# Graph layers on one Trainium2 core: each chunk's products right behind its copied sums, its bias added beside the square, and new limits for where conversions are placed

## The chip, the cores and the metric

The kernel runs on one core of a Trainium2 chip. A core has five engines with queues of their own, each worked off in order: TensorE (PE, matrix products into PSUM), VectorE (DVE), ScalarE (ACT), GpSimd (POOL), and SyncE (SP), which here only issues DMA transfers. Engines wait for each other by semaphores. The metric is the device time of one execution in microseconds (us), the median of several runs.

## The reference, cut to what matters

```python
# x: 4096 x 64; adj: 4096 x 4096, mostly zero, with the diagonal set
h = relu(layernorm(x))
for k in range(2):                       # first layer, two hops
    agg = adj @ h
    h = tanh(concat([agg, h], 1) @ W[k])
x = x + h

h = relu(layernorm(x))                   # second layer
support = h @ weight
mask = adj != 0
rank = cumsum(mask, axis=1); deg = rank[:, -1:]
k = minimum(deg, 100); pos = rank - (deg - k)
w = mask * where(pos > 0, 0.5 ** (k - pos), 0)
out = x + w @ support + bias
```

The adjacency is needed as numbers three times: in the first hop, in the second hop, and as the weights w of the second layer, which depend only on where its nonzeros stand.

## The kernel before, in words

The 4096 nodes are 32 blocks of 128, and the blocks make four chunks (numbered 0 to 3) of eight. A 512 KB block of the adjacency is 128 source nodes by the 1024 target nodes of a chunk, in fp32.

**First sweep** (`sweep1`, until about 202 us). All blocks are loaded; PE sums the first hop, and VectorE and ScalarE turn each block into one byte per entry ("codes"), from which the weight of the second layer can be computed later. A code becomes final when the counts of its row are known; `settle` (L392, L396) subtracts them for four blocks at once.

**Second sweep** (`sweep2`, L756). The second hop needs 72 of the blocks again. They go through a ring of six slots of one block, from the 21st block on through four (L803 to L806). SyncE issues the transfer of a block (L814) when PE has given up its slot, and PE adds it with two products (`agg_pair`, L256). The 36 steps of the loop take two blocks each: four of chunk 2, eight of chunk 3 (blocks 5 to 12), twelve of chunk 2 (13 to 24), 24 of chunk 1 (25 to 48), 24 of chunk 0 (49 to 72). `lasts` names the last block of each chunk. Then `finish_x2` (L536) makes the input of the second layer from a chunk's sums, in stages that are separated by `yield`:

1. ScalarE copies the sums from PSUM (S, L540), and SyncE loads the residual (xres, L542);
2. PE multiplies S by the hop's weights (py, L548), VectorE adds the other half (y, L554), ScalarE takes tanh (L558);
3. VectorE adds the residual (L561) and forms mean and difference (L189, L190), ScalarE squares (L191);
4. VectorE sums the squares (L193, L194), and GpSimd takes the power of -0.5 (L195);
5. VectorE scales (L198) and splits the result in a high and a low half (L582, L583), which are the features; GpSimd adds the bias for the output to `pre1` (L587).

Beside this runs **the second layer** in 128 units. A unit is a conversion of one block of codes into fp32r weights and two products with the features (`layer1`, L695). ScalarE converts with one instruction (Exp, L656) and VectorE with two (L648, L651). A conversion needs a free buffer for its weights, and takes one that an earlier unit has given up; at first there are only a few. The units of chunk 3 come first, then those of chunks 2, 1 and 0. Full sums are moved out of PSUM into `parts` (L724, L727, L730), and at the end multiplied by the layer's weight and added to `pre1` (`finish_out`, L746, L751), and stored (L753).

**What sets the order.** The order on each engine is written out when the program is built. A planner keeps a clock for each engine, in us, with a fixed cost for each operation (`use`). `chain` holds the chunk that is being finished and the time of its next stage; `run_chain` issues a stage once PE's clock has reached that time. `decode` (L660) places conversions on ScalarE as long as its clock is less than `lead` (5.0) ahead of PE's, on VectorE up to `dlead`, and settles in between. Where a chunk is being finished and more than three converted blocks are in stock, a conversion has to end within 0.4 of the chunk's next stage. `fill` and the loop's end place units where their features and weights are ready by the clocks. The last 56 units stand behind the last block (`n_late`), with the finishing of chunk 0 among them.

Of the kernel before, what the change touches and what calls it, by code (L numbers as in the profile page):

```python
# [16 lines left out]
ALU = mybir.AluOpType  # L17
AX = mybir.AxisListType

P = 128  # L20
# [23 lines left out]
def gnn_kernel(  # L44
# [20 lines left out]
    nc = tc.nc  # L65

    D = x.shape[-1]
# [3 lines left out]
    CB = 8  # L71
# [26 lines left out]
    pre1 = cpool.tile([P, NB, D], F32, name="pre1")  # L98
# [44 lines left out]
    bias_b = wb[:, HOPS * 2 + 1, :]  # L143
# [240 lines left out]
    settled = []  # L384
# [112 lines left out]
    clock = {"PE": 0.0, "DVE": 0.0, "ACT": 0.0, "POOL": 0.0, "DMA": 0.0}  # L497

    def use(engine, us, after=0.0):
        clock[engine] = max(clock[engine], after) + us  # L500
        return clock[engine]
# [33 lines left out]

    def finish_x2(I, acc):  # L536

        h = chunk(I)
        S = tmp(name="S")
        nc.scalar.copy(S, acc)  # L540
        xres = tmp([P, CB, D], name="xres")
        nc.sync.dma_start(xres, x[I])  # L542
        yield use("ACT", 0.6, clock["PE"] + 0.2) + 0.1

        pt = one(name="py")
        v = by_t(S)
        for t in range(TC):
            nc.tensor.matmul(  # L548
                pt[:, t * P : (t + 1) * P].rearrange("p (c e) -> p c e", c=NC),
                v[:, t // 2, t % 2, :], wz[:, :, 1, 0, :],  # L550
                start=True, stop=True, skip_group_check=True,
            )
        y = tmp([P, CB, D], name="y")
        nc.vector.tensor_tensor(  # L554
            as_nodes(y), pt.rearrange("p (t c e) -> p t c e", t=TC, c=NC), as_nodes(pre1[:, h, :]),
            op=ALU.add,
        )
        nc.scalar.activation(y, y, AF.Tanh)  # L558
        t = use("DVE", 0.7, use("PE", 1.15) + 0.2)
        yield use("ACT", 0.65, t + 0.1) - 0.5  # L560
        nc.vector.tensor_add(pre1[:, h, :], xres, y)  # L561
        t = use("DVE", 0.7, clock["ACT"] + 0.1)
        ln = ln_relu(None, pre1[:, h, :])
        next(ln)
        t = use("DVE", 1.4, t)
        yield use("ACT", 0.65, t + 0.1)
        next(ln)
        t = use("DVE", 0.9, clock["ACT"])
        yield use("POOL", 1.8, t + 0.1)
        try:  # L570
            next(ln)
        except StopIteration as stop:
            h2 = stop.value
        t = use("DVE", 0.9, clock["POOL"])
        if I == NCH - 1:
            feats[I] = feats[1] = place([P, CB, 2 * D], F32R, "mbuf", "feat")
        elif I == 0:
            feats[I] = feats[2]
        assert I > 1 or state["done"] >= CB * NCH * (2 - I)
        assert I != 2 or not any(w is lent[2] for w, _ in made[state["done"] :])  # L580
        hi, lo = feats[I][:, :, :D], feats[I][:, :, D:]
        nc.vector.tensor_scalar(hi, h2, SCALE, None, op0=ALU.mult)  # L582
        nc.vector.scalar_tensor_tensor(  # L583
            lo, h2, SCALE, hi.bitcast(F32), op0=ALU.mult, op1=ALU.subtract
        )
        ready[I] = use("DVE", 1.2, t + 0.1) + 0.2
        nc.gpsimd.tensor_tensor(  # L587
            pre1[:, h, :], pre1[:, h, :],
            bias_b[:, None, :].to_broadcast([P, CB, D]), op=ALU.add,
        )  # L590

# [29 lines left out]
    units = [(J, g, n) for J in range(NCH - 1, -1, -1) for g in order[J] for n in range(CB)]  # L623
    sums = {}
    parted = set()
    ready = {}
    made = []
    done = {}
    chain = []
    state = {"done": 0, "lead": 5.0, "dve": False, "dlead": 1.0, "free": 0.0}  # L630

    def convert(engine=None):
        i = len(made)
# [26 lines left out]
    def decode():  # L660
        while True:
            ahead = len(made) - state["done"]
            now = clock["PE"] + state["lead"]

            end = max(chain[0][0], clock["PE"]) + 0.4 if chain and ahead > 3 else 1e9
            t = min((v[1] for v in spaces), default=1e9)
            act, dve = (max(clock[e], t) for e in ("ACT", "DVE"))
            if len(made) == len(units):
                act = dve = 1e9
            if state["dve"] and dve + 1.4 < act + 1.05 and dve <= min(max(clock["PE"] + state["dlead"], state["free"]), end - 1.4):  # L670
                convert("DVE")
            elif act <= min(now, end - 1.05):
                convert("ACT")
            elif settled and clock["DVE"] <= clock["PE"] + 1.5 and (
                not chain or max(clock["DVE"], clock["PE"]) <= max(chain[0][0], clock["PE"]) + 0.3
            ):
                J, g, s = settled[0]
                settle()
                done[J, g] = use("DVE", 1.25)
            else:  # L680
                return

    def layer1(n):

        for i in range(state["done"], min(state["done"] + n, len(units))):
            state["done"] += 1
            while len(made) <= i:
                convert()
            J, g, k = units[i]
            if k == 0 and g not in sums:  # L690
                sums[g] = pacc.tile([P, NC, C], F32, tag="acc", name="accl")
            first, last = k == 0 and (J + 1, g) not in kept, k == CB - 1 and (J, g) not in kept
            w = made[i][0]
            for c in range(NC):
                nc.tensor.matmul(  # L695
                    sums[g][:, c, :], feats[J][:, k, :], w[:, c * C : (c + 1) * C],
                    start=first, stop=last,
                )
            space(w, use("PE", 0.45, max(made[i][1], ready[J])) + 0.2)
            if k < CB - 1:  # L700
                continue
            t = clock["PE"] + 0.2

            if (J, g) == (NCH - 1, 1):

                give_back("bits")
                state["dve"] = True
            if 0 < J < NCH - 1 or J and g % 2:
                pair_space(f"code{g}{J}", t)
            elif J:  # L710
                parts[g // 2] = place([P, 2, NC, C], F32, f"code{g}{J}", "parts")
            if (J, g) in kept:
                continue
            t = evict(J, g, sums.pop(g))
            if J == 0:
                outs.append((t + 0.1, partial(finish_out, g, part(g))))
# [39 lines left out]
    def sweep2(acc):  # L756
# [8 lines left out]
        free = {s: 3.5 * (n // 2 - 2) for n, s in enumerate(ring_all)}  # L765
# [7 lines left out]
        def run_chain(now):  # L773
            if chain and chain[0][0] <= now:
                t, gen = chain.pop(0)
                t = next(gen, None)
                if t is not None:
                    chain.insert(0, (t, gen))
                return True
            return False  # L780
# [20 lines left out]
        for n in range(0, total, 2):  # L801
            I, b = blocks[n]
            if n == 20:  # L803
                slots = ring_all[2:4] + ring_all[:2]
                seq = 0
                pair_space(f"ring{rings[2]}", *(free[s] for s in ring_all[4:]))  # L806
            if I not in accs:
                accs[I] = two(name="acc1") if I == 1 else plow.tile([P, C], F32, tag="low", name="acc1")
            fill(slots[seq % len(slots)])
            for r in range(2):  # L810
                s = slots[seq % len(slots)]
                seq += 1
                a = ring[s[0]][:, s[1], :]
                nc.sync.dma_start(a, adjA[I, NB - 1 - b - r])  # L814
                landed = use("DMA", 1.33, free[s]) + 2.2
                agg_pair(accs[I], at(b + r)[:, D:], a, (I, b + r) == firsts[I], (I, b + r) == lasts[I])
                free[s] = use("PE", 0.9, landed)
            next(last, None)
            if (I, b) == (2, NB - 2):
                give_back(I)  # L820
            if (I, b + 1) == lasts[I]:
                gen = finish_x2(I, accs[I])
                chain.append((next(gen), gen))
            run_chain(clock["PE"])
            if I == 0:

                state["lead"] = min(10.0, 1.1 * (total - 3 - n))
            decode()
            while state["done"] < min(due(n + 2) + 6, len(units) - n_late):
                i = state["done"]  # L830
                J = units[i][0]
                if J not in ready or max(ready[J], made[i][1] if len(made) > i else 1e9) > clock["PE"] + 0.3:
                    break
                layer1(1)
                run_chain(clock["PE"])
                decode()
# [64 lines left out]
```

## Time and profile before

| | |
|---|---|
| median of three runs | 372.81 us (371.53 to 374.83) |
| profiled execution, its own time | 370.68 us |
| span of its instructions | 368.8 us |
| PE busy | 338.8 us (92%) |
| VectorE busy | 293.0 us (79%) |
| ScalarE busy | 200.9 us (54%) |
| GpSimd busy | 24.6 us (7%) |
| DMA | 108.45 MB, mean 294 GB/s |
| granted TensorE clock | 1.0 |

The profile is of one execution. A row of the timeline gives start and length in us, engine, source line, operation, what it writes and reads with shape and type, how many instructions were merged, and in brackets how long the engine was idle before and what ended that. PE's fp32 products are recorded twice each: x4 of L256 is one block. Ends of PE's rows are modelled and overlap the next start a little, so the time of work in a run is taken from start to start. A row of the waits gives the engine and line that waited, what released it, and the sum, number and longest of these waits.

### The profile page before, as it was taken

The numbers are of one execution on the slowest core, as the hardware profiler recorded it, in microseconds if no ns is written. First come the engines' busy times: TensorE is split into PE (matmuls) and PEld (weight loads), VectorE is DVE, ScalarE is ACT, GpSimd is POOL, SyncE is SP. The second block draws the span as 40 slices with busy tenths as digits, with TensorE's granted clock in tenths as the row PEclk, the third lists the DMA queues.
The fourth block names the chain that finished last, engine by engine and source line by source line (L and its number), as shares of the span: only waits on it lengthen the run. The fifth ranks groups of instructions, "written<-read, shape, count | busy, mean of one in ns | idle before, by whom it ended". The sixth has DMA issues, their size and how long they took to land. (4 is left out here: it accounts for less than half of the span.)

```text
span 368.8 us, 3974 instructions
## 1 busy us (share of the span) xinstructions
PE 338.8 (92%) x1356; PEld 151.4 (41%) x1356; DVE 293.0 (79%) x522; ACT 200.9 (54%) x227; POOL 24.6 (7%) x21
## 2 busy tenths in 40 slices
PE   3787789999999999999999989799999999989996
PEld 0142224333343444534444422143355534447585
DVE  4998999399989999979989866688458629948993
ACT  2277981675167350650002424158969499939991
POOL 2221100000000000000000000312000030003000
PEclk9999999999999999999999999999999999999999
DMA  8999999999995978739999889978985698820002
GB/s 300 411 410 406 407 410 406 411 410 407 409 400 150 378 297 334 287 121 367 294 306 350 314 299 412 336 283 305 311 303 184 226 335 283 289 96 0 2 29 85
DMA packets 29827, 108.45 MB, mean 294 GB/s; under 512 B 2416, under 2 KB 2800, under 8 KB 29808
## 3 DMA queue, kind: packets, MB, share of 16 engines
q1 hardware_dynamic: 29808, 108.21, 79.3%
q8 instruction: 10, 0.16, 0.2%
q14 instruction: 9, 0.07, 0.0%
HBM read 107.15 MB, written 1.05 MB: 293 GB/s over the span
## 5 line engine op out<-in xcount | busy, mean ns | idle before, releaser
L656 ACT ACTIVATE weights<-codes,zero 128x1024 fp32r<-128x1024 uint8 x93 | 98.5, 1138 | 5.7 <-PE accl L695 5.2
L256 PE MATMUL acc<-ring,hx 128*64 128x512 f32 x288 | 71.6, 608 | 8.8 <-DMA ring<-in_adjA_dram 8.6
L695 PE MATMUL accl<-weights,feat 128*128 128x512 f32 x254 | 67.6, 407 | 1.4 <-DVE weights L651 1.0
L468 PE MATMUL acc<-ring,hx 128*128 128x512 f32 x152 | 66.1, 593 | 0.0
L256 PE MATMUL acc_low<-codes,hx 128*64 128x512 f32 x224 | 53.4, 598 | 7.9 <-DMA codes<-in_adjA_dram 7.9
L695 PEld LDWEIGHTS accl<-weights,feat 128*128 128x128 f32 x254 | 44.9, 188 | 29.2 <-ACT weights L656 13.4
L468 PEld LDWEIGHTS acc<-ring,hx 128*128 128x128 f32 x152 | 28.7, 190 | 37.1 <-issue 36.5
L250 DVE TENSOR_SCALAR cnt<-codes 128x512 uint16<-128x512 uint16 x128 | 37.7, 294 | 4.4
L249 DVE TENSOR_TENSOR codes<-mbuf,cnt 128x512 uint16<-128x512 uint16 x90 | 38.4, 427 | 3.1
L195 POOL TENSOR_TENSOR s<-s,half 128x8 f32<-128x8 f32 (+2 forms) x9 | 17.6, 1956 | 306.7 <-DVE s L194 306.7
L256 PEld LDWEIGHTS acc<-ring,hx 128*64 128x64 f32 x288 | 16.7, 135 | 51.3 <-DMA ring<-in_adjA_dram 28.1
L396 DVE TENSOR_TENSOR codes<-codes,after 128x2048 uint16<-128x2048 uint16 x32 | 37.7, 1219 | 0.0
L230 ACT ACTIVATE codes<-codes 128x1024 uint8<-128x1024 int8 x32 | 33.8, 1057 | 1.0
L238 DVE TENSOR_SCALAR mbuf<-ring 128x2048 uint8<-128x2048 f32 x27 | 32.9, 1220 | 1.0 <-DMA ring<-in_adjA_dram 1.0
L256 PE MATMUL acc_low<-ring,hx 128*64 128x512 f32 x96 | 25.5, 643 | 8.0 <-DVE hx L198 6.3
L229 ACT ACTIVATE codes<-codes 128x1024 int8<-128x1024 f32 x24 | 25.1, 1046 | 11.5 <-DMA codes<-in_adjA_dram 11.5
L256 PEld LDWEIGHTS acc_low<-codes,hx 128*64 128x64 f32 x224 | 15.2, 136 | 39.0 <-issue 23.1
L651 DVE TENSOR_SCALAR weights<-bits 128x1024 fp32r<-128x1024 f32 x34 | 23.6, 694 | 6.6 <-PE accl L695 3.6
L238 DVE TENSOR_SCALAR mbuf<-codes 128x2048 uint8<-128x2048 f32 x21 | 25.6, 1220 | 0.0
L648 DVE TENSOR_SCALAR bits<-codes 128x1024 uint32<-128x1024 uint8 x34 | 23.5, 692 | 0.8
L289 ACT CAST mbuf<-mbuf 128x1024 bf16<-128x1024 uint8 x1 | 1.0, 1045 | 37.9 <-DVE mbuf L288 37.9
L468 PE MATMUL acc<-codes,hx 128*128 128x512 f32 x40 | 17.8, 595 | 0.0
(87 smaller groups left out, 238.1 us busy)
## 6 DMA issues: line engine op xcount, KB each, us to landing
ring<-in_adjA_dram SPq DMA_DIRECT2D x74, 512.0 KB, 4.8
codes<-in_adjA_dram SPq DMA_DIRECT2D x33, 1024.0 KB, 15.5
ring<-in_adjA_dram SPq DMA_DIRECT2D x30, 1024.0 KB, 5.4
pre<-in_x_dram SPq DMA_DIRECT2D x4, 256.0 KB, 6.3
xres<-in_x_dram SPq DMA_DIRECT2D x4, 256.0 KB, 5.7
out_dram<-o SPq DMA_DIRECT2D x3, 256.0 KB, 2.5
out_dram<-o SPq DMA_DIRECT2D x2, 128.0 KB, 2.0
wb<-in_weights_dram SPq DMA_DIRECT2D x1, 192.0 KB, 17.4
```

Of the source, the lines that this page charges most:

```text
L229: nc.scalar.activation(sign, a[:, r], AF.Sign)
L230: nc.scalar.activation(m, sign, AF.Square, scale=float((FLAG - 1 + 0.25) ** 0.5))
L238: nc.vector.tensor_scalar(m, a, 0.0, float(FLAG - 1), op0=ALU.not_equal, op1=ALU.mult)
L249: nc.vector.tensor_tensor(q, marks[r].bitcast(U16), cnt, op=ALU.add)
L250: nc.vector.tensor_scalar(cnt, q, 0x7F7F, None, op0=ALU.bitwise_and)
L256: nc.tensor.matmul(acc[c * D : (c + 1) * D, :], src, a[:, c * C : (c + 1) * C], start=first, stop=last,)
L396: nc.vector.tensor_tensor(q, q, a[:, None, :].to_broadcast([P, 4, CW // 2]), op=ALU.subtract)
L468: nc.tensor.matmul(acc[0][:, c, :], at(g), a[:, r, c * C : (c + 1) * C], start=g == CB * I - 1, stop=g == 0,)
L648: nc.vector.tensor_scalar(state["bits"], q, float(ZERO), ONE, op0=ALU.subtract, op1=ALU.mult)
L651: nc.vector.tensor_scalar(w, state["bits"].bitcast(F32), 2.0 ** (127 - LOW), None, op0=ALU.mult)
L656: nc.scalar.activation(w, q, AF.Exp, scale=LN2, bias=zero)
L695: nc.tensor.matmul(sums[g][:, c, :], feats[J][:, k, :], w[:, c * C : (c + 1) * C], start=first, stop=last,)
```

## The change

It has five parts. (1) When the last block of a chunk is in the queue, and it isn't chunk 0's, the loop goes on with the chunk at once: two units if the next ones are ready, and then the stage with py, ahead of any further block. (2) The bias is added in stage 3, behind the difference and so beside the square, no longer in stage 5; the planner's cost of GpSimd's power goes from 1.8 to 2.5. (3) Each stage names two gaps, one for VectorE and one for ScalarE: how far behind the stage's time a conversion may still end. They take the place of the one limit of 0.4. (4) A settle needs to end 0.1 us plus VectorE's gap behind that time, where it had to begin by 0.3 behind it. (5) `dlead` is 2.0 from the start instead of 1.0.

```diff
     def finish_x2(I, acc):
...
-        yield use("ACT", 0.6, clock["PE"] + 0.2) + 0.1
+        state["gap"] = 1.35, 2.2
+        t = use("ACT", 0.6, clock["PE"] + 0.2) + 0.1
+        yield t
...
-        t = use("DVE", 0.7, use("PE", 1.15) + 0.2)
+        t = use("DVE", 0.7, use("PE", 1.15, t) + 0.2)
+        state["gap"] = 0.6, 2.7
         yield use("ACT", 0.65, t + 0.1) - 0.5
...
         t = use("DVE", 1.4, t)
+        nc.gpsimd.tensor_tensor(
+            pre1[:, h, :], pre1[:, h, :],
+            bias_b[:, None, :].to_broadcast([P, CB, D]), op=ALU.add,
+        )
+        state["gap"] = 0.0, 1e9
         yield use("ACT", 0.65, t + 0.1)
...
-        yield use("POOL", 1.8, t + 0.1)
+        yield use("POOL", 2.5, t + 0.1)
...
         ready[I] = use("DVE", 1.2, t + 0.1) + 0.2
-        nc.gpsimd.tensor_tensor(
-            pre1[:, h, :], pre1[:, h, :],
-            bias_b[:, None, :].to_broadcast([P, CB, D]), op=ALU.add,
-        )
...
-    state = {"done": 0, "lead": 5.0, "dve": False, "dlead": 1.0, "free": 0.0}
+    state = {"done": 0, "lead": 5.0, "dve": False, "dlead": 2.0, "free": 0.0, "gap": (0.0, 0.0)}
...
-            end = max(chain[0][0], clock["PE"]) + 0.4 if chain and ahead > 3 else 1e9
+            d_end, a_end = (
+                max(chain[0][0], clock["PE"]) + g + 0.1 if chain else 1e9 for g in state["gap"]
+            )
+            idle = clock["DVE"] <= clock["PE"] + 1.5 and max(clock["DVE"], clock["PE"]) + 1.25 <= d_end
+            if ahead <= 3:
+                d_end = a_end = 1e9
...
-            if state["dve"] and dve + 1.4 < act + 1.05 and dve <= min(max(clock["PE"] + state["dlead"], state["free"]), end - 1.4):
+            if state["dve"] and dve + 1.4 < act + 1.05 and dve <= min(max(clock["PE"] + state["dlead"], state["free"]), d_end - 1.4):
                 convert("DVE")
-            elif act <= min(now, end - 1.05):
+            elif act <= min(now, a_end - 1.05):
                 convert("ACT")
-            elif settled and clock["DVE"] <= clock["PE"] + 1.5 and (
-                not chain or max(clock["DVE"], clock["PE"]) <= max(chain[0][0], clock["PE"]) + 0.3
-            ):
+            elif settled and idle:
...
                 gen = finish_x2(I, accs[I])
                 chain.append((next(gen), gen))
+                if len(chain) == 1 and n < total - 2:
+                    if made and units[state["done"]][0] in ready and ready[units[state["done"]][0]] < clock["PE"] + 0.3:
+                        layer1(2)
+                    run_chain(chain[0][0])
             run_chain(clock["PE"])
```

## The prediction

> **What bounds the kernel now.** First the windows view: what each engine does in four stretches of the second half (it starts near 202 us; the changed steps all lie there).
>
> ```profile
> 202.00:240.00 38.00, 32.84 (x143) 10.42 (x142) 26.86 (x30) 12.08 (x19) 3.77 (x2) 1.00 0.93 339
> 240.00:290.00 50.00, 48.53 (x205) 23.65 (x204) 33.39 (x43) 38.99 (x40) 3.79 (x2) 1.00 0.80 269
> 290.00:328.50 38.50, 36.35 (x149) 15.31 (x148) 26.61 (x41) 29.44 (x30) 3.21 (x2) 1.00 0.79 274
> 328.50:368.80 40.30, 35.62 (x181) 27.80 (x179) 30.32 (x46) 30.98 (x31) 2.91 (x2) 1.00 0.08 27
> ```
>
> The columns after the length are PE, PE's weight loads, VectorE, ScalarE, GpSimd, granted clock, DMA share and GB/s. PE is busy 32.8 of 38, then 48.5 of 50, then 36.4 of 38.5. It is the bound, and its amount of work is fixed: the change leaves PE's instructions the same in number. So the only thing to win is PE's idle time, and the timeline of PE tells where it lies:
>
> ```profile
> 218.88 1.08 PE L256 MATMUL acc<-ring,hx 128*64 128x512 f32 x4 [0.75 <-DMA ring<-in_adjA_dram]
> 220.82 1.08 PE L256 MATMUL acc<-ring,hx 128*64 128x512 f32 x4 [0.86 <-DMA ring<-in_adjA_dram]
> 223.12 1.21 PE L548 MATMUL py<-wz,S 128*128 128x128 f32 x8
> 235.82 1.08 PE L256 MATMUL acc<-ring,hx 128*64 128x512 f32 x4 [1.22 <-DMA ring<-in_adjA_dram]
> 237.80 1.08 PE L256 MATMUL acc<-ring,hx 128*64 128x512 f32 x4 [0.90 <-DMA ring<-in_adjA_dram]
> 240.04 1.21 PE L548 MATMUL py<-wz,S 128*128 128x128 f32 x8
> ```
>
> One L256 x4 is one 512 KB block of the adjacency. From the end of chunk 3's last block (219.96) to 240 PE waits for blocks in eleven gaps, 4.42 us together; later come 0.29, 0.49, 0.53, 0.15 (248 to 267 us), 0.73 (301.55), and 1.24 and 0.17 before the last two blocks (325, 326). In the tail, after the last block, it waits for converted weights:
>
> ```profile
> 340.00 2.00 PE L695 MATMUL accl<-weights,feat 128*128 128x512 f32 x6 [0.16 <-ACT weights L656]
> 342.26 1.20 PE L695 MATMUL accl<-weights,feat 128*128 128x512 f32 x4 [0.26 <-DVE weights L651]
> 343.72 2.72 PE L695 MATMUL accl<-weights,feat 128*128 128x512 f32 x10 [0.26 <-DVE weights L651]
> 346.78 3.31 PE L695 MATMUL accl<-weights,feat 128*128 128x512 f32 x12 [0.34 <-DVE weights L651]
> ```
>
> With 0.18 at 355.5 that is 1.20 us. Last, SyncE's waits: nearly every transfer waits until PE has given up its slot, so PE's order also sets when blocks arrive.
>
> ```profile
> SPq L814 <- PE acc L256: 82.9, 64, 4.5
> ```
>
> **What the Trainium skill says.** "Perfetto Trace Analysis", Optimization Strategy: find the gaps on the contended engine, what each waits for, and let that start sooner. The trace fits, with the gaps above. "DMA: Bandwidth & Descriptors", Anatomy of one DMA, fits about 2.0 us + bytes/436 GB/s (for another issuing path): an estimate of 3.2 us for a block. The trace has 3.26 (issued 244.95, landed 248.21), and 1.24 to 1.28 us from landing to landing in a full queue (221 to 233 us). "SBUF — State Buffer", SBUF: two separate sides, says that a VectorE operation with two SBUF inputs and a GpSimd operation share a port pair that one of them holds whole. The trace agrees:
>
> ```profile
> 232.90 1.75 DVE L198 SCALAR_TENSOR_TENSOR xc<-xc,s 128x512 f32<-128x512 f32 x1 [0.39 <-POOL s L195]
> 305.46 0.68 DVE L198 SCALAR_TENSOR_TENSOR xc<-xc,s 128x512 f32<-128x512 f32 x1
> 232.83 1.26 POOL L587 TENSOR_TENSOR pre<-pre,wb 128x512 f32<-128x512 f32 x1
> ```
>
> L198 takes 1.75 us beside the bias addition L587 and 0.68 without it.
>
> **The change, part by part.** I walk the queues of the changed kernel in their built order with durations of this trace: a block 0.935 us in a run (a pair 1.87), n units of layer 1 in a row 0.18 + 0.47n (66 ns off at most for 1, 3, 6 and 9 units), a py group 1.14, a conversion on ScalarE 1.045, a settle on VectorE 1.2.
>
> *Products right behind the sums, chunk 3.* ScalarE copies S 0.1 us after the last block (219.96; so it was at 220.06), in 0.58; py starts at about 220.75 instead of 223.12. PE waits 0.8 us for it. Block 13 starts 1.07 later than before, but landings are 1.28 apart and blocks take 0.935, so PE has caught up by block 17. SyncE reissues the slots of blocks 13 and 14 up to 1.0 us later; its queue holds four transfers then, so no landing moves. The chain on VectorE and ScalarE (y, tanh, sum, mean, square, power, features) then ends at 231.8 instead of 235.83: 2.4 from py, 0.6 from two settles that stood inside it, 1.07 from L198.
>
> *Units earlier.* Seven units now stand between blocks 22 and 23, at 233.3, when the features are ready. They fill the gaps of 1.22 and 0.90. But there are only five weight buffers, so the fifth to eleventh conversions wait for the first to seventh of these units: the first is read out at 233.9, seven conversions later it is 241.35. In ScalarE's built order all seven stand **ahead of the copy of S for chunk 2**, whose last block ends at 238.65. PE has two units to do (to 239.75), and then py stands at its head waiting for S until 242.1: a **new wait of 2.35 us**. Three units and chunk 1's blocks queue behind it, and SyncE's transfers wait for their slots. Sum from 219.96 to the end of block 26: 0.8 + about 1.1 for blocks 17 to 22 + 2.35 = 4.25 against 4.42. No gain yet, though seven units are done ahead.
>
> *240 to 290.* One unit stands ahead of blocks 27 and 28 and three ahead of 29 to 32, where before only one unit stood between them; of the gaps of 1.46 about 0.5 is left (block 32). Behind chunk 1's last block the copy of S has two conversions ahead of it and two units cover it: 0.3. Units come in 26 groups instead of 21 up to the last py: 5 x 0.18 = 0.9 us more. But each DMA wait also costs PE a refill (1.04 us of this stretch is neither work nor listed idle), and most of this goes with the waits. Walked: with 48 blocks, 45 units and py, PE stands at 286.65, plus 0.4 for what refill remains, against 289.94 less two blocks, 288.07: **1.0 us ahead**.
>
> *290 to py of chunk 0.* The order is two blocks and two or three units in turn, without the run of four blocks that cost 0.73. The last four blocks still stand in a row: 1.41 stays. **0.7 us.** Body: 1.7 us, with 0.9 if all refill stays and 2.3 if none does.
>
> *Gaps and leads of the planner.* They add no instruction. Five conversions go from VectorE to ScalarE, and in the tail 28 + 10 stand behind the last S instead of 29 + 11. Two conversions more in stock, where the two engines make 0.96 + 0.69 per us, are 1.2 us of supply: as much as the five waits of the tail. I take **1.0 us** of it; the ends are 0 (other waits come up) and 1.2.
>
> *Bias beside the square.* It was behind the power on GpSimd and is now ahead: 1.26 us from the end of xc, while square and second sum need about 1.6, so the power isn't held up. How L193 runs beside it, no row shows: between 0 and 1.26 us more, against 1.07 saved at L198. I take 0 for L193. For the end both count nothing: chunk 3's features have 1.5 us to spare, those of chunks 2 and 1 over 6 (units that need them come at 270 and 309), those of chunk 0 are covered by 22 units (10.6 us). Without that cover the loss would be 0.2 at most. The residual's loads keep their place in SyncE's order.
>
> Sum: 1.7 + 1.0 = **2.7 us less**. The profiled execution took 370.68 (span 368.8 and 1.9 around it), so 368.0; on the median of the runs, 372.81, it is **370.1**.
>
> **Rivals.**
> - *ScalarE isn't in the way.* If conversions ahead of chunk 2's S end by 239 (units start earlier, or buffers come free sooner), the 2.35 goes too: 5.1 us, 367.7. For it: ScalarE had 5.9 us of idle before that copy. Against: the five buffers and the built order.
> - *The gain stays in the ring.* Filled gaps return as block waits, since the blocks behind the seven units are fetched later (slots of 23 and 24 come free at 237.7 instead of 234.6): only part of the tail is left, 0.5 us, 372.3. For it: the 82.9 us above. Against: four blocks need 5.4 us through four slots (0.37 from release to issue, 3.26 to landing, 1.6 for the second of a pair, 1.08 on PE, less 0.93), and PE has work of 6.4 for four blocks with two and three units.
> - *Slower: py blocks PE behind ScalarE's backlog.* The planner lets ScalarE run 5.0 us ahead. If that is its backlog at the copies of chunks 2 and 1, PE stands 5.2 us at each, 8.0 more than I count: 5.3 slower, 378.1. It decides from 2.7 us of stalls beyond mine. For it: a copy can't pass conversions. Against: at chunk 1's copy the buffers are in use until PE's units just before, so the backlog can't be that long.
>
> **How the numbers follow.** Forecast 0.50 (369.2 to 372), first rival 0.22, second 0.16, third 0.12. About 1% is what a measurement of this kernel can tell from no change. Faster by over 1% (under 369.1): the first rival and 0.06 of the forecast, 0.28. Slower by over 1% (over 376.5): 0.10 of the third. The rest 0.62. The range takes in the first rival with 0.9 more body gain (366.8) and the second, with a slip of 1.7 where stalls grow a little (374.0).
>
> **What would show it.** Right: py of chunk 3 at about 220.8, its features by 232, PE idle of 2 us before py of chunk 2 with ScalarE's conversions as releaser, L198 near 0.7 everywhere, the last py near 326.7, under 0.4 us of waits between 339 and 356. Wrong: no wait at that py, or waits of over 4 us at two of them, or block waits after 243 above 3 us.

## The result, and the profile after

The changed kernel takes 368.77 us (median of 20 runs, 367.31 to 372.12), the kernel before, run beside it, 372.41 (20 runs). The measured ratio is 0.9922, 95% interval 0.9896 to 0.9949: **0.8% less, 2.9 us** (1.9 to 3.9). The two medians are 3.6 us apart, which lies inside this interval; the text goes by the ratio. Two repetitions beside the experiments gave 0.9941 (0.9917 to 0.9965) and 0.9921 (0.9900 to 0.9942). The forecast was 2.7 us, a time of 370.1. The profiled execution has a span of 365.7 us, against 368.8.

First the windows view of the changed kernel, cut at its own last py (columns as in the view of before: length, PE, weight loads, VectorE, ScalarE, GpSimd, clock, DMA share, GB/s).

```profile
202.00:240.00 38.00, 35.31 (x153) 13.29 (x152) 27.28 (x31) 17.23 (x24) 3.82 (x2) 1.00 0.92 328
240.00:290.00 50.00, 47.38 (x199) 21.37 (x198) 33.23 (x46) 39.69 (x41) 3.84 (x2) 1.00 0.81 281
290.00:326.00 36.00, 34.74 (x141) 14.06 (x140) 20.20 (x32) 28.33 (x29) 2.93 (x2) 1.00 0.83 293
326.00:365.70 39.70, 35.83 (x184) 28.49 (x182) 27.93 (x44) 30.68 (x31) 2.94 (x2) 0.98 0.08 27
```

PE does 2.5 us more in the first stretch and 1.1 less in the second; what moved is where the work stands. PE's timeline shows all its gaps of 0.3 us and more after chunk 3's last block, and two rows without a gap (326.62 and 327.47) that mark the last py and the start of the tail:

```profile
220.99 1.21 PE L551 MATMUL py<-wz,S 128*128 128x128 f32 x8 [0.74 <-ACT S L541]
242.34 1.21 PE L551 MATMUL py<-wz,S 128*128 128x128 f32 x8 [1.95 <-ACT S L541]
...
323.19 1.08 PE L256 MATMUL acc<-ring,hx 128*64 128x512 f32 x4 [0.95 <-DMA ring<-in_adjA_dram]
324.57 1.08 PE L256 MATMUL acc<-ring,hx 128*64 128x512 f32 x4 [0.30 <-DMA ring<-in_adjA_dram]
326.62 1.10 PE L551 MATMUL py<-wz,S 128*128 128x128 f32 x8
327.47 15.67 PE L703 MATMUL accl<-weights,feat 128*128 128x512 f32 x64
343.44 2.81 PE L703 MATMUL accl<-weights,feat 128*128 128x512 f32 x10 [0.31 <-ACT weights L661]
346.56 0.73 PE L703 MATMUL accl<-weights,feat 128*128 128x512 f32 x2 [0.30 <-ACT weights L661]
```

The gaps of 1.22 and 0.90 before blocks 24 and 25 are gone, and in their place PE stands 1.95 us before chunk 2's py. ScalarE's timeline shows why: the seven conversions that wait for buffers of the first units come before the copy in its queue.

```profile
234.43 1.15 ACT L661 ACTIVATE weights<-codes,zero 128x1024 fp32r<-128x1024 uint8 x1 [1.42 <-PE accl L703]
235.49 1.14 ACT L661 ACTIVATE feat<-codes,zero 128x1024 fp32r<-128x1024 uint8 x1
236.53 4.25 ACT L661 ACTIVATE weights<-codes,zero 128x1024 fp32r<-128x1024 uint8 x4
240.69 1.13 ACT L661 ACTIVATE feat<-codes,zero 128x1024 fp32r<-128x1024 uint8 x1
241.72 0.56 ACT L541 COPY S<-acc 128x512 f32<-128x512 f32 x1
```

SyncE still waits mostly for PE to give up slots, in its row of the waits (sum, number, longest):

```profile
SPq L822 <- PE acc L256: 82.2, 65, 6.3
```

The bias addition runs beside the square and the second sum. From VectorE's and GpSimd's timelines:

```profile
226.59 0.69 DVE L193 TENSOR_REDUCE s<-sq 128x8 f32<-128x512 f32 x1 [0.76 <-ACT sq L191]
230.15 0.69 DVE L198 SCALAR_TENSOR_TENSOR xc<-xc,s 128x512 f32<-128x512 f32 x1 [0.40 <-POOL s L195]
231.34 0.69 DVE L592 SCALAR_TENSOR_TENSOR feat<-xc,feat 128x512 fp32r<-128x512 f32 x1
...
226.01 1.27 POOL L570 TENSOR_TENSOR pre<-pre,wb 128x512 f32<-128x512 f32 x1 [183.05 <-DVE xc L190]
227.56 2.55 POOL L195 TENSOR_TENSOR s<-s,half 128x8 f32<-128x8 f32 x1 [0.28 <-DVE s L194]
```

L193 keeps its 0.69 us beside the addition, L198 has 0.69 instead of 1.75, and chunk 3's features end at 232.0. One limit of these readings: three profiled executions of the changed kernel have spans of 365.7, 368.4 and 366.8 us. From the last py to the end they agree (39.12, 39.15, 39.12), but the last py stands at 326.6, 329.2 and 327.7: the second sweep starts at 202.5, 203.5 and 202.0, and from there to the last py they take 124.1, 125.7 and 125.6, with other landings of blocks. So the tail is read from traces, and for the body the timed ratios decide.

### The profile page after: what moved, and what is told of

Its sections match the earlier page's. It is cut to its first block, busy times and chain, and to the rows that moved or that the text cites. A ratio compares the mean times of both kernels' runs of the same rounds, so it can differ in the third digit from the quotient of the medians.

```text
span 365.7 us, 3966 instructions
## 1 busy us (share of the span) xinstructions
PE 340.6 (93%) x1356; PEld 151.9 (42%) x1356; DVE 284.2 (78%) x514; ACT 205.3 (56%) x230; POOL 24.1 (7%) x21
## 4 chain that ended last, share of the span: by engine, by line
PE 73%; DMA 15%; ACT 5%; SPq 4%; issue 2%; DVE 0%; ACTq 0%
PE acc L468 23%; PE acc L256 16%; PE accl L703 15%; PE acc_low L256 10%; DMA codes<-in_adjA_dram 9%; DMA ring<-in_adjA_dram 6%; SPq L428 3%; PE po L208 3%; PE pto L754 2%; PE pt L324 2%; ACT weights L661 2%; PE py L551 1%; ACT codes L229 1%; PE pt L319 1%; ACT codes L230 1%
## 5 line engine op out<-in xcount | busy, mean ns | idle before, releaser
L661 ACT ACTIVATE weights<-codes,zero 128x1024 fp32r<-128x1024 uint8 x96 | 101.6, 1136 | 13.7 <-PE accl L703 10.4
L703 PEld LDWEIGHTS accl<-weights,feat 128*128 128x128 f32 x250 | 43.9, 188 | 31.0 <-ACT weights L661 15.0
L256 PE MATMUL acc_low<-ring,hx 128*64 128x512 f32 x96 | 27.4, 692 | 7.7 <-DVE hx L198 6.3
L656 DVE TENSOR_SCALAR weights<-bits 128x1024 fp32r<-128x1024 f32 x29 | 20.1, 694 | 9.9 <-PE accl L703 4.4
L570 POOL TENSOR_TENSOR pre<-pre,wb 128x512 f32<-128x512 f32 x4 | 5.1, 1281 | 270.6 <-DVE xc L190 270.6
L653 DVE TENSOR_SCALAR bits<-codes 128x1024 uint32<-128x1024 uint8 x29 | 20.0, 690 | 0.6
```

Source lines behind the costliest of these rows:

```text
L256: nc.tensor.matmul(acc[c * D : (c + 1) * D, :], src, a[:, c * C : (c + 1) * C], start=first, stop=last,)
L653: nc.vector.tensor_scalar(state["bits"], q, float(ZERO), ONE, op0=ALU.subtract, op1=ALU.mult)
L656: nc.vector.tensor_scalar(w, state["bits"].bitcast(F32), 2.0 ** (127 - LOW), None, op0=ALU.mult)
L661: nc.scalar.activation(w, q, AF.Exp, scale=LN2, bias=zero)
L703: nc.tensor.matmul(sums[g][:, c, :], feats[J][:, k, :], w[:, c * C : (c + 1) * C], start=first, stop=last,)
```

## The experiments

My theory had three parts: PE's idle time is filled by units that are ready earlier because of chunk 3's early features; the new wait at chunk 2's py costs 2 us of that; the tail is set by the conversions that are left behind the last copy of sums. The rivals were that another part of the change carries the gain, that the ring takes it back, and that PE's own work sets the tail. The first four experiments ran beside the kernel before alone, the later ones beside the changed kernel too. "Body" is from the sweep's first block to the last py, "tail" from there to the end of the span (before: 126.2 and 40.4 us; after: 124.1 and 39.1 in the first trace).

**One part alone: the direct products.** The kernel before with this, and with the planner's wait for the copy as in the change:

```diff
                 gen = finish_x2(I, accs[I])
                 chain.append((next(gen), gen))
+                if len(chain) == 1 and n < total - 2:
+                    if made and units[state["done"]][0] in ready and ready[units[state["done"]][0]] < clock["PE"] + 0.3:
+                        layer1(2)
+                    run_chain(chain[0][0])
             run_chain(clock["PE"])
```

> The kernel before with one part of the change alone: the products py stand right behind the copied sums of chunks 3, 2 and 1 (part 1, with the planner's wait for the copy). Bias, gaps, settles and leads are as before. In its built order no units stand between blocks 22 and 23, two units cover the copy of chunk 2's sums, and 38 conversions stand behind the last copy. My theory (PE's idle time is filled by units that are ready earlier, and the tail is shortened by two more conversions in stock): the gap of 1.2 us before block 24 stays, most later ones go, body 1.0 us shorter, tail 1.0 us shorter, 2 us less than before (ratio 0.995). Rival 1 (the gaps of the planner carry the gain): no change, ratio 1.000. Rival 2 (the early products are everything): 2.9 us less, ratio 0.992.

Measured: ratio 0.997 (0.9948 to 0.9993), 1.1 us less: the sign of my theory, and half its size; both rivals lie outside the interval. The tail is 38.8 us, 1.6 less than before, with 38 conversions left. So the body gained nothing (126.8 us in the trace). PE's timeline of this run, and ScalarE's, show where it went:

```profile
236.87 1.08 PE L256 MATMUL acc<-ring,hx 128*64 128x512 f32 x4 [1.24 <-DMA ring<-in_adjA_dram]
288.07 1.21 PE L549 MATMUL py<-wz,S 128*128 128x128 f32 x8 [2.30 <-ACT S L540]
```

```profile
273.92 13.63 ACT L657 ACTIVATE weights<-codes,zero 128x1024 fp32r<-128x1024 uint8 x13
287.46 0.56 ACT L540 COPY S<-acc 128x512 f32<-128x512 f32 x1
```

The gap before block 24 stayed, and chunk 1's py now waits 2.30 us for a copy behind thirteen conversions in a row. Without the other parts, the third rival's mechanism (py behind ScalarE's backlog) comes in at chunk 1.

**One part alone, and undone: the bias.** In the first kernel the bias addition stands ahead of the square and all else is as before; in the second it stands behind the features again and all else is as after.

```diff
         t = use("DVE", 1.4, t)
+        nc.gpsimd.tensor_tensor(
+            pre1[:, h, :], pre1[:, h, :],
+            bias_b[:, None, :].to_broadcast([P, CB, D]), op=ALU.add,
+        )
```

> The kernel before with the bias addition moved ahead of the square and nothing else; the order on PE, ScalarE and SyncE stays. My theory: L198 falls from 1.75 to 0.69 us in three of the four chunks, nothing moves up to the last py, and in the tail VectorE's conversions start 1.07 us earlier, which is worth about 0.5 us (between 0 and 0.8): ratio 0.9985. Rival (this move makes the whole gain of the tail): 1.3 us less, ratio 0.9965. Other rival (the addition holds up the second sum beside it): no change, with L193 near 1.3 us.

Measured: ratio 0.9997 (0.9969 to 1.0026), tail 40.2 us, 0.2 less than before.

> The changed kernel with the bias addition back behind the power, its planner's costs and so every other queue unchanged. My theory: the body stays 2 us shorter than before, the tail loses about 0.5 us against the changed kernel, so 2.4 us less than before (ratio 0.9935). Rival (the move of the bias makes the tail's gain of 1.3 us): 1.6 us less, ratio 0.9957.

Measured: ratio 0.9899 (0.9864 to 0.9934), tail 39.14 us, as with the bias beside the square. L198 is back at 1.75 us (1.78 in the tail) in three chunks. So the move does to L198 what was expected, and is worth 0.2 us of tail where 40 conversions are left and nothing that can be seen where 38 are. My 0.5 us was too much, and the rival's 1.3 is out. In the first of the two kernels a settle of VectorE ran beside chunk 3's addition, which then took 2.10 us instead of 1.27 and held the power up: it started 1.33 us after L193's start, against 0.96 before and 0.97 in the changed kernel. So there L198's 1.06 us was gained only in part.

**Moved to another queue: the copy of chunk 2's sums.** All other places in the queues are those of the changed kernel.

```diff
-        nc.scalar.copy(S, acc)
+        (nc.vector.tensor_copy if I == 2 else nc.scalar.copy)(S, acc)
```

> The changed kernel with the copy of chunk 2's sums on VectorE in place of ScalarE, the planner's clocks and every other place in the queues unchanged. VectorE's settles end at 237.7 us, so the copy isn't behind ScalarE's conversions. My theory (PE waits 1.95 us at the second py because the copy stands behind seven conversions): that wait falls to about 0.3, later blocks and units come about 1.7 us earlier, and the whole is 4.6 us less than before (ratio 0.9877). Rival (the wait is made up later in any case, since weights or ring slots are the limit there): the wait goes but other waits of 1.5 us come between 243 and 260 us, 3 us less than before (ratio 0.992).

Measured: ratio 0.9847 (0.9807 to 0.9888); the wait at the second py is gone, and the rival's 0.992 lies outside the interval. From the timelines of VectorE and PE in the repetition of this run, in which py follows its two units without a gap:

```profile
239.40 0.69 DVE L541 COPY S<-acc 128x512 f32<-128x512 f32 x1 [1.68 <-PE acc L256]
```

```profile
239.28 1.20 PE L703 MATMUL accl<-weights,feat 128*128 128x512 f32 x4
240.32 1.10 PE L551 MATMUL py<-wz,S 128*128 128x128 f32 x8
```

But in its first trace only 0.4 of the 2.3 us at this py were left at the last py, against the changed kernel's first trace; block waits had come instead. So it was run again beside the changed kernel.

> The changed kernel once more, for comparison with the next three on the same chip: ratio 0.992 to the kernel before. Both theories expect the same.

Measured: 0.9941 (0.9917 to 0.9965), 2.2 us less than before.

> The changed kernel with the copy of chunk 2's sums on VectorE, once more beside the changed kernel. In its first trace the second py came 2.3 us earlier, but the last py only 0.4 us earlier, since block waits came back. Theory A (the slots of the ring take the gain back): 0.4 us less than the changed kernel, ratio to before 0.991. Theory B (those block waits were late landings of that one execution): 1.5 us or more less than the changed kernel, ratio 0.988 or lower.

Measured: 0.9876 (0.9846 to 0.9907), 4.6 us less than before and 2.4 less than the changed kernel by the ratios on this chip. The two times of this kernel (5.7 and 4.6 us less) are about that of the forecast's first rival (5.1), brought about by another edit. Theory B holds: the block waits differ from one execution to the next. The bodies fit: 123.7 and 124.1 us in this kernel's two traces, against 124.1, 125.7 and 125.6 in the changed kernel's three, so the first comparison was with a short one. In the repetition the longest is at block 33:

```profile
256.42 1.08 PE L256 MATMUL acc<-ring,hx 128*64 128x512 f32 x4 [2.12 <-DMA ring<-in_adjA_dram]
```

**The tail: more conversions left.** The changed kernel with VectorE's lead at 1.0.

```diff
-    state = {"done": 0, "lead": 5.0, "dve": False, "dlead": 2.0, "free": 0.0, "gap": (0.0, 0.0)}
+    state = {"done": 0, "lead": 5.0, "dve": False, "dlead": 1.0, "free": 0.0, "gap": (0.0, 0.0)}
```

> The changed kernel with VectorE's lead back at 1.0 from the start (part 5 undone). In its built order 42 conversions stand behind the last copy of sums, where the changed kernel has 38 and the kernel before 40; the order up to block 32 is unchanged. My theory (the tail is set by the conversions that are left then, 1.65 per us of both engines together): from the last py to the end 39.1 + 4/1.65 = 41.5 us, 2.4 more than the changed kernel; body unchanged; 0.5 us less than before in all (ratio 0.9985). Rival (the tail is set by PE's own work or by the chunk's chain): the tail stays at 39.1 us, ratio 0.992.

Measured: ratio 1.0013 (0.9984 to 1.0042), and a tail of **41.56 us** for the 41.5 expected. PE waits for weights six times now, 0.30 or 0.31 us each, as these rows of its timeline show:

```profile
337.63 0.73 PE L703 MATMUL accl<-weights,feat 128*128 128x512 f32 x2 [0.30 <-ACT weights L661]
338.67 1.77 PE L703 MATMUL accl<-weights,feat 128*128 128x512 f32 x6 [0.31 <-ACT weights L661]
340.75 2.82 PE L703 MATMUL accl<-weights,feat 128*128 128x512 f32 x10 [0.31 <-ACT weights L661]
```

From start to start such a wait costs more than its bracket: the unit at 337.63 takes 1.04 us to the next row, where a unit in a row takes 0.47. Four waits more than the changed kernel's two make up about 2.3 of the 2.4 us. These explain most of the loss against the changed kernel (0.7% between the two ratios, 2.7 us). So the change without part 5 gains nothing that can be measured (1.0013, interval to both sides of 1): the longer tail takes what the body gains.

**The tail: less work for PE in it.** Two units go between the last pairs of blocks, into the gap of 0.95; the copy of chunk 2's sums is on VectorE as above.

```diff
+            if n == total - 4:
+                layer1(2)
         for k in rings[:2]:
             pair_space(f"ring{k}", free[k, 0], free[k, 1])
```

> The kernel with the copy on VectorE, and in addition two units between the last two pairs of blocks, where PE waits 1.0 us for a block; so two units fewer stand behind the last py, and still 38 conversions. Theory A (conversions set the tail): the wait goes, the last py comes about as before, the tail has 0.9 us more of waits for weights or is the same: no gain over the same kernel without this edit (within 0.3 us). Theory B (PE's work sets the tail): 0.9 us less than that kernel.

Measured: ratio 0.9845 (0.9808 to 0.9881), tail 39.13 us: the same tail, with two units less in it. PE waits longer in exchange:

```profile
331.84 9.02 PE L703 MATMUL accl<-weights,feat 128*128 128x512 f32 x36 [0.93 <-DVE parts L732]
341.17 2.81 PE L703 MATMUL accl<-weights,feat 128*128 128x512 f32 x10 [0.30 <-ACT weights L661]
344.28 0.73 PE L703 MATMUL accl<-weights,feat 128*128 128x512 f32 x2 [0.31 <-ACT weights L661]
```

These waits are 1.54 us, 0.93 more than the changed kernel's 0.61, about the time of the two units. The longest isn't for weights: VectorE moves full sums out of PSUM (L732) behind chunk 0's chain, and PE needs that place. But the first wait for weights ends 16.83 us after the last py here (341.17) and 16.82 in the changed kernel (343.44). The conversions come at the same time, and PE only stands earlier. So PE's work doesn't set the tail. The whole times can't decide this: the 0.3% between this ratio and that of the same kernel without the two units (0.9876) is 1.1 us, the size of Theory B, but inside the intervals. From chunk 1's py to the last py the trace has 41.5 us and that of the repetition 42.3, against 42.0 and 41.4 without the two units, so the saving isn't seen there either.

**Which chunks need the direct products.** The condition in the loop was narrowed: not for chunk 2 in one kernel (shown), for chunk 3 alone in the other (`I == 3 and` in the same place).

```diff
-                if len(chain) == 1 and n < total - 2:
+                if I != 2 and len(chain) == 1 and n < total - 2:
```

> The changed kernel, for comparison with the next three on the same chip: ratio 0.993 to the kernel before, body (first block of the sweep to last py) near 124.5 us, tail 39.1.

Measured: 0.9921 (0.9900 to 0.9942).

> The changed kernel without the products right behind the sums for chunk 2 alone; chunks 3 and 1 have them. In the built order three units, two blocks and one unit stand between chunk 2's last block and its py, and 38 conversions behind the last copy. My theory (what gains is chunk 3's early features; at chunk 2 the direct products only make PE wait 1.95 us for the copy): no wait at the second py, body 1.0 to 1.5 us shorter than the changed kernel's, tail 39.1 us, ratio to before 0.989. Rival (chunk 2's early products are part of the gain): 0.5 us or more longer than the changed kernel.

Measured: ratio 0.986 (0.9818 to 0.9901), 2.3 us less than the changed kernel by the ratios, tail 39.12. All six runs (366.29 to 367.29) lie below all 22 of the changed kernel beside them (367.38 to 371.27). PE's timeline: three units, two blocks and one unit cover the copy, and py follows without a wait.

```profile
238.75 1.66 PE L703 MATMUL accl<-weights,feat 128*128 128x512 f32 x6
240.34 1.94 PE L256 MATMUL acc<-ring,hx 128*64 128x512 f32 x8
242.20 0.73 PE L703 MATMUL accl<-weights,feat 128*128 128x512 f32 x2
242.77 1.10 PE L551 MATMUL py<-wz,S 128*128 128x128 f32 x8
```

Counted from the sweep's first block this py starts later than in the changed kernel (at 41.0 us, against 39.8, 40.4 and 40.6 in its three traces), and the kernel is faster: PE has worked instead of standing.

> The changed kernel with the products right behind the sums for chunk 3 alone. In the built order chunk 1's py stands two blocks and two units later, 39 conversions stand behind the last copy. My theory (chunk 1's features are early enough in any case, they are not needed before the 64th unit): as with the direct products kept at chunk 1 up to the last py, the tail 0.6 us longer for one conversion more: ratio 0.9905. Rival (chunk 1's early products are part of the gain): 0.5 us or more longer than the changed kernel.

Measured: ratio 0.988 (0.9833 to 0.9926), tail 39.8 us with 39 conversions left (0.7 more than with 38, for 0.6 expected). Chunk 1's direct products aren't part of the gain by this run; its interval is too wide to say that they cost nothing.

> The kernel with the copy of chunk 2's sums on VectorE and two units between the last pairs of blocks, once more: ratio to before 0.986, 2 us or more less than the changed kernel on the same chip; tail 39.1 us.

Measured: 0.987 (0.9827 to 0.9912), tail 39.13, 1.9 us less than the changed kernel by the ratios.

The tails together:

| kernel | conversions behind the last copy | tail, us | ratio to before |
|---|---|---|---|
| products direct, alone | 38 | 38.8 | 0.997 |
| the change | 38 | 39.1 | 0.992 (0.994, 0.992) |
| the change, bias back | 38 | 39.1 | 0.990 |
| copy of chunk 2 on VectorE | 38 | 39.1 | 0.985 (0.988) |
| the same, units between the last pairs | 38 | 39.1 | 0.985 (0.987) |
| not direct for chunk 2 | 38 | 39.1 | 0.986 |
| direct for chunk 3 alone | 39 | 39.8 | 0.988 |
| bias first, alone | 40 | 40.2 | 1.000 |
| before | 40 | 40.4 | 1 |
| the change, lead 1.0 | 42 | 41.6 | 1.001 |

From 38 to 42 conversions the tail grows by 2.4 us, 0.61 each, which is the 1.65 per us that both engines make together. The number alone isn't exact: the kernel with 38.8 has one conversion less on ScalarE and one more on VectorE than the others with 38.

Three edits of the changed kernel beat it and the kernel before: the copy of chunk 2's sums on VectorE (medians 366.1 and 366.4 us), the same with units between the last pairs (365.7 and 367.2), and no direct products for chunk 2 (366.6). All three take away the wait at the second py. Their intervals overlap, so no order among them is given. The kernel with direct products for chunk 3 alone (367.6) has no such wait either, but its interval overlaps the changed kernel's.

No run takes out the new limits of the planner (parts 3 and 4) by themselves, or has them alone. That they, with part 1, bring the seven units between blocks 22 and 23 is argued by elimination: the seven stand there also with the bias moved back and with the lead at 1.0, and part 1 alone puts none there. What the limits are worth in time stays open. Nor does a run leave out the direct products of chunk 3 alone: that the body's gain comes from chunk 3's early features is argued from the filled gaps in the traces and from the kernel in which chunk 3 alone has them (0.988).

## Why the prediction was right

- **Total.** Forecast 2.7 us, measured 2.9 (2.2 and 2.9 in the repetitions). The case that came true is the forecast's own, by its mechanism: the wait at chunk 2's py came. The median, 368.77, is just below that case's 369.2 to 372, since the kernel before was 0.4 us faster here than in the forecast and the medians lie 3.6 us apart. That the sum is so close is in part luck: the body was probably put too high and the tail too low.
- **Products behind the sums, chunk 3.** PE waited 0.74 us for the copy, forecast 0.8; PE caught up with the landings at block 17, as walked; the features ended at 232.0 (forecast 231.8).
- **The new wait.** Forecast 2.35 us by counting seven conversions ahead of the copy; measured 1.95: PE came to this py at 240.39 (walked: 239.75) and began it at 242.34 (walked: 242.1). That the wait isn't made up later is shown by two different edits that remove it: 2.4 and 2.3 us less than the changed kernel by the ratios, each uncertain by about 1.5 us. The first rival gave 5.1 us for the kernel without this wait, and with the copy on VectorE 4.6 and 5.7 were measured; in the change itself ScalarE was in the way, as the forecast had it.
- **The body.** 1.7 us forecast. The first trace shows 2.1, but single traces differ by that much, so the ratios decide: 2.2 to 2.9 us in all, less 1.26 of tail, is 0.9 to 1.6. So the term was probably a little large, though the intervals don't exclude 1.7. That the last py stood at 326.6 as forecast is luck: it stood at 329.2 and 327.7 in the other traces. The saved refills were put too high. Redone with the walk's own durations, the stretch from 240.04 to 288.80 before (24 blocks, 45 units in 11 groups, one py, 1.47 us of gaps) leaves 0.6 us that is neither work nor listed idle, not 1.04; the same stretch after (242.34 to 285.58) leaves 0.4. So about 0.2 us went, where 0.6 was counted.
- **The tail.** 1.0 us forecast, 1.26 measured: I held part of the supply back for waits that didn't come. Which part of the change brings the two conversions was wrong: the forecast put them to the planner's gaps and leads, but part 1 alone already leaves 38, and without part 5 the rest leaves 42. The mechanism, conversions left behind the last copy, is the best shown of all: 41.56 for 41.5 in the run with 42, and 39.13 with two units less for PE. PE's waits in the tail were 0.61 us, not under 0.4 as I wrote.
- **The bias.** Counted as nothing for the end: 0.0 to 0.2 us of tail measured. L193 wasn't held up, as I had taken for it.
- **Rivals.** The ring's rival failed: it left 0.5 us of gain, and the interval begins at 1.9 (1.3 in the first repetition). Block waits after 243 us are 1.9, 2.6 and 2.9 us in the three traces, against 3.6 in the one before; but 3 us was a poor sign for "wrong", since the faster kernel with the copy on VectorE has 3.4 and 4.1. The slower rival failed for the change as a whole, since ScalarE's backlog is short at chunk 1; with the direct products alone it is long there (2.30 us of wait), and takes the body's gain.

## What to carry to other kernels

A step that PE takes "at once" stands at PE's head until its input is there, so before it is moved up, count what is queued ahead of the producer of that input on its engine: here seven conversions turned an earlier py into 2 us of standing, and letting PE do other work first was faster though py came later. Where two engines feed a last stretch, count the feeds that are left when it begins and divide by their joint rate: that gave the change of the tail to 0.1 us in three kernels, and missed by 0.3 where the split between the engines differed. Filling a gap on the bounding engine with work that is due anyway doesn't pay by itself: two units in the gap of 0.95 left the tail as long as it was, since the conversions came no earlier.

## What the runs showed of the hardware

The same transfer in the same program can take very different times. Block 33 in the kernel with the copy on VectorE was issued (end of the issuing instruction) at 249.78 and landed at 253.78 us in one execution, 4.0 us; in another it was issued at 250.18 and landed at 256.38, 6.2 us, and PE waited 2.12 us for it. The block ahead of it had landed at 251.66 and 252.06, so the backlog doesn't explain the 2.2 us. The block waits after 243 us of one kernel differ by 1.0 us (changed kernel) to 1.9 us (1.1 and 3.0, units between the last pairs) between executions, and a body difference of that size can't be read from one trace. A copy of 128x512 from PSUM on ScalarE, on which PE waits with nothing before it, cost PE 0.74 us in each of the traces in which chunk 3's products stand right behind it; the copy itself took 0.58 or 0.59. GpSimd's power on 128x8 took 2.55 us beside two settles of VectorE and 1.65 beside none (both in the changed kernel).
